# A gated graph network and an attention layer on one core: the weight setup in pieces among the first pair's work

## The chip, the cores and the metric

The kernel runs on one core of a Trainium2 chip. The metric is the time of one execution on the device in microseconds (us). Before the change it is 2468.5 us, the median of 3 runs (2468.18 to 2470.1). Five engines work beside each other, each in its own order: TensorE (PE) multiplies, VectorE (DVE) and ScalarE (ACT) work elementwise, GpSimd (POOL) does a few elementwise operations here, and SyncE (SP) issues DMAs. An engine waits at an instruction until what it needs from the others is there, and everything behind it on that engine waits too.

## The reference

There are 64 graphs of 256 nodes, with 256 features each. Layer 0 takes h = relu(layernorm(x)) and runs a gated recurrent cell three times; then x becomes x plus the last h:

```python
for i in range(3):
    m = h @ weight[i]                      # 256 x 256
    aggr = einsum('bst,bsd->btd', adj != 0, m)
    gi = aggr @ w_ih.T + b_ih ; gh = h @ w_hh.T + b_hh
    r = sigmoid(i_r + h_r) ; z = sigmoid(i_z + h_z)
    n = tanh(i_n + r * h_n)
    h = (1 - z) * n + z * h
```

Layer 1 is a graph attention with four heads on relu(layernorm(x)): a linear map W, b; logits from two attention vectors per head with a leaky relu; a mask where adj is not 1; a softmax over the row; a product with the mapped features; and a second residual.

## The kernel before

A pair is two graphs, 512 nodes; there are 32 pairs. Features lie on the 128 partitions in two halves, k or c = 0 and 1. For each of the three steps of layer 0 the kernel gathers h along the edges (`gather`, L444), and multiplies h with the hidden weights and the gathered sums s with one matrix that holds message weight and input weight together (`product`, L464, called as rA, rB, zA, zB, nhA, nhB, niA, niB). The matmuls run in a fast float format, fp32r, and to keep precision each operand is split in parts: for activations a leading part (`h_hi`, `s_hi`, on ACT), a rest (`h_lo` on POOL, `s_lo` on DVE) and a difference (`h_d`, `s_d`, on DVE); for weights the parts a, bS (the rest times 4096) and b-a. An A product takes the parts a and bS, a B product the part b-a. The gates then follow: `lift` copies the A product on ACT, `join` adds the B product on DVE, `squash` is the tanh; `addA`, `addB`, `new`, `diff` (POOL), `mixz` and `state` form the next h.

The order of the work is written out by hand. `PLAN` gives each operation of a pair a place, pairs follow each other at 74.0 (`PERIOD`), and all operations are emitted in the order of their places. There is no scheduler: on each engine the instructions stand in this order. Two or three pairs are under way at any time.

Ahead of all pairs stands the setup (L180 to L277). It loads the weights on ACT's DMA queue, transposes w_ih and w_hh on PE (L204, copies at L205), splits the hidden weights (`in_halves`, L183 to L193), then for each of the three steps transposes the message weights (L218), multiplies them with w_ih in plain fp32 (L224), copies the product to SBUF (L228) and splits it. At the end it makes the weights and biases of layer 1 (L259 to L275). The two tiles of layer 1's map are w_val and b_val. Setup's tiles lie in a pool of their own, which is closed at L277; the pools `sb` and `small`, with nearly all tiles of the pairs, are opened after that and take the same space. So the first pair's load of x (L311) waits for setup's last readers there. PSUM is one pool of 8 banks, taken in turn by all products and transposes, setup's too.

Of the kernel before, what the change touches and what calls it, by code (L numbers as in the profile page):

```python
# [17 lines left out]
P = 128  # L18
# [8 lines left out]
S = 4096.0  # L27
# [78 lines left out]


@with_exitstack
def gated_gnn_then_gat_kernel(
# [60 lines left out]

    setup_scope = ExitStack()
    setup = setup_scope.enter_context(tc.tile_pool(name="setup", bufs=1))

# [6 lines left out]
    w_msg = setup.tile([P, L, KD, D], F32, name="w_msg")  # L180
    nc.scalar.dma_start(w_msg, weight.rearrange("l (k q) e -> q l k e", q=P))

    def in_halves(full, name):  # L183

        a = const.tile([P, KD, G * P], F32R, name=f"a_{name}")
        b = setup.tile([P, KD, G * P], F32, tag="b", name=f"b_{name}", bufs=2)
        bs = const.tile([P, KD, G * P], F32R, name=f"bs_{name}")
        ba = const.tile([P, KD, G * P], F32R, name=f"ba_{name}")
        nc.scalar.mul(a, full, TRIM)
        nc.vector.tensor_sub(b, full, a)  # L190
        nc.scalar.mul(bs, b, S)
        nc.vector.scalar_tensor_tensor(ba, a, -1.0 / S, b, op0=ALU.mult, op1=ALU.add)
        return {"a": a, "bS": bs, "b-a": ba}  # L193

    wT, gates = {}, {}
    for name, src in (("ih", w_ih), ("hh", w_hh)):
        nat = setup.tile([P, G, D], F32, name=f"{name}_nat")
        nc.scalar.dma_start(nat, src.rearrange("(g q) d -> q g d", q=P))
        wT[name] = setup.tile([P, KD, G * P], F32, name=f"{name}_T")
        for k in range(KD):  # L200
            for g0 in range(0, G, 3):
                pt = bank(f"pw_{name}_{k}_{g0}")
                for g in range(3):
                    nc.tensor.transpose(pt[:, ts(g, P)], nat[:, g0 + g, ts(k, P)], ident)  # L204
                nc.vector.tensor_copy(wT[name][:, k, g0 * P : (g0 + 3) * P], pt[:, : 3 * P])  # L205

    for k in range(KD):
        nc.scalar.mul(wT["hh"][:, k, 2 * D :], wT["hh"][:, k, 2 * D :], 0.5)
    gates["h"] = in_halves(wT["hh"], "hh")


    for l in range(L):
        w_in = setup.tile([P, KD, G * P], F32, tag="w_in", name=f"w_in_{l}", bufs=2)
        msgT = setup.tile([P, KD, D], F32, tag="msgT", name=f"msgT_{l}", bufs=2)
        for e in range(KD):
            pt = bank(f"pmT_{l}_{e}")
            for d in range(KD):
                nc.tensor.transpose(pt[:, ts(d, P)], w_msg[:, l, d, ts(e, P)], ident)  # L218
            nc.scalar.copy(msgT[:, e, :], pt[:, :D])
        for d in range(KD):  # L220
            for g0 in range(0, G, 3):
                pt = bank(f"pwi_{l}_{d}_{g0}")
                for e in range(KD):
                    nc.tensor.matmul(  # L224
                        pt[:, : 3 * P], msgT[:, e, ts(d, P)], wT["ih"][:, e, g0 * P : (g0 + 3) * P],
                        start=(e == 0), stop=(e == KD - 1),
                    )
                nc.vector.tensor_copy(w_in[:, d, g0 * P : (g0 + 3) * P], pt[:, : 3 * P])  # L228
        gates[l] = in_halves(w_in, f"in{l}")

    bi = const.tile([P, G], F32, name="bi")
    bh = const.tile([P, G], F32, name="bh")
    nc.scalar.dma_start(bi, b_ih.rearrange("(g q) -> q g", q=P))
    nc.scalar.dma_start(bh, b_hh.rearrange("(g q) -> q g", q=P))
    nc.vector.tensor_scalar_mul(bh[:, 2 * KD :], bh[:, 2 * KD :], 0.5)

    brz = const.tile([P, 2 * KD], F32, name="brz")
    nc.vector.tensor_add(brz, bi[:, : 2 * KD], bh[:, : 2 * KD])
    nc.vector.tensor_scalar_mul(brz, brz, 0.5)

    w_nat = setup.tile([P, KD, D], F32, name="w_nat")
    nc.scalar.dma_start(w_nat, W.rearrange("(k q) d -> q k d", q=P))
    bcol = const.tile([P, KD], F32, name="bcol")
    nc.scalar.dma_start(bcol, b.rearrange("(k q) -> q k", q=P))

    a_exp = setup.tile([P, KD, 2 * H], F32, name="a_exp")
    nc.vector.memset(a_exp, 0.0)
    for h in range(H):
        k, q0 = divmod(h * C, P)
        for s in range(2):  # L250
            nc.scalar.dma_start(
                a_exp[q0 : q0 + C, k, s * H + h : s * H + h + 1],
                a[h : h + 1, s * C : (s + 1) * C].rearrange("o c -> c o"),
            )
    w_val = const.tile([P, KD, VW], F32, name="w_val")
    for k in range(KD):
        pt = bank(f"pwv_{k}")
        for g in range(KD):
            nc.tensor.transpose(pt[:, ts(g, P)], w_nat[:, g, ts(k, P)], ident)  # L259
        nc.vector.tensor_copy(w_val[:, k, :D], pt[:, :D])  # L260
        pa = bank(f"pwa_{k}")
        for g in range(KD):
            nc.tensor.matmul(
                pa[:, : 2 * H], w_nat[:, g, ts(k, P)], a_exp[:, g, :], start=(g == 0), stop=(g == KD - 1)
            )
        nc.vector.tensor_copy(w_val[:, k, D:], pa[:, : 2 * H])
    b_val = const.tile([P, VW], F32, name="b_val")
    nc.scalar.dma_start(b_val[:, :D], bass.AP(tensor=b.tensor, offset=b.offset, ap=[[0, P], [1, D]]))
    bmat = setup.tile([P, KD, P], F32, name="bmat")
    pb = bank("pb")  # L270
    for k in range(KD):
        nc.vector.tensor_copy(bmat[:, k, :], bcol[:, k : k + 1].to_broadcast([P, P]))
    for k in range(KD):
        nc.tensor.matmul(pb[:, : 2 * H], bmat[:, k, :], a_exp[:, k, :], start=(k == 0), stop=(k == KD - 1))
    nc.vector.tensor_copy(b_val[:, D:], pb[:, : 2 * H])  # L275

    setup_scope.close()  # L277
    sb = ctx.enter_context(tc.tile_pool(name="sb", bufs=2))
    small = ctx.enter_context(tc.tile_pool(name="small", bufs=3))
# [11 lines left out]
    class Pair:  # L291
# [26 lines left out]
        def reload(self):  # L318
            p = self.p
            self.x1 = sb.tile([P, R, D], F32, tag="x1", name=f"x1_{p}")  # L320
            nc.sync.dma_start(self.x1, x_rows[ts(p, T), :].rearrange("(r q) d -> q r d", q=P))
# [136 lines left out]
        def product(self, name, kind, sources, g):  # L458

            pt = bank(f"p{name}_{self.p}")  # L460
            pairs_ = (("a", "a"), ("bS", "b")) if kind == "A" else (("b-a", "d"),)
            parts = [(w[v], x, half, k) for w, x in sources for k in range(KD) for v, half in pairs_]
            for j, (w, x, half, k) in enumerate(parts):
                nc.tensor.matmul(  # L464
                    pt, w[:, k, ts(g, P)], self.halves[x, half, k], start=(j == 0), stop=(j == len(parts) - 1)
                )
            return pt
# [81 lines left out]
        def valadd(self, r):  # L549
            self.val = self.once("val", lambda: sb.tile([P, R, VW], F32, tag="val", name=f"val_{self.p}"))  # L550
            nc.vector.tensor_add(self.val[:, r, :], self.ps_["v", r][:, :VW], b_val)
# [7 lines left out]
        def srow(self):  # L559
            self.srow_ = tile_of("o", f"srow_{self.p}", bufs=1)  # L560
            nc.scalar.copy(self.srow_[:H, :], self.prow[:H, :])
# [5 lines left out]
        def rows(self, i):  # L567
            self.rows_[i] = sb.tile([P, H, N], F32, tag="rows", name=f"rows_{self.p}_{i}", bufs=1)
            src = self.line_[:, ts(i, N)]
            nc.sync.dma_start(self.rows_[i], bass.AP(tensor=src.tensor, offset=src.offset, ap=[[0, P], [T, H], [1, N]]))  # L570


        def slope(self, i, s):
            p, r = self.p, i * KN + s
            self.zz[r] = sb.tile([P, H, N], F32, tag="zz", name=f"zz_{p}_{r}")
# [39 lines left out]
        def prcopy(self, i, s, j):  # L615
            self.prT[i] = self.once(
                ("prT", i), lambda: sb.tile([P, KN, H, N], F32, tag="prT", name=f"prT_{self.p}_{i}", bufs=1)
# [17 lines left out]
        def ocopy(self, i):  # L635
            self.oT[i] = sb.tile([P, H // 2, N], F32, tag="oT", name=f"oT_{self.p}_{i}", bufs=1)
            nc.scalar.copy(flat(self.oT[i]), self.ps_["o"])
# [9 lines left out]
        def scale(self, i):  # L647
            self.o[i] = tile_of("o", f"o_{self.p}_{i}", bufs=1)
# [20 lines left out]
    todo = sorted(  # L669
        ((p * PERIOD + place, j, q, name, args) for p, q in enumerate(pairs) for j, (place, name, *args) in enumerate(PLAN)),  # L670
        key=lambda x: x[:2],
    )
    with tc.manual_schedule():
        for _, _, q, name, args in todo:
            if name[-1] in "AB" and name[:-1] in ("r", "z", "nh", "ni"):
                q.gate(name[:-1], name[-1], *args)
            else:
                getattr(q, name)(*args)
# [30 lines left out]
```

## Time and profile before

| | us |
|---|---|
| median of 3 runs | 2468.5 |
| the profiled execution, own time | 2469.03 |
| its span, first to last instruction | 2467.2 |
| PE busy | 2389.7 (97%) |
| DVE busy | 2111.5 (86%) |
| ACT busy | 1858.3 (75%) |
| POOL busy | 720.0 (29%) |

A page of the profile gives the busy time of each engine, the span in 40 slices with the clock that PE was granted, the DMA queues, the chain of work that ended last, and the costliest groups of instructions. A group's row names the line, the engine and the operation, what is written from what, the count, the busy time and the mean in ns, and the idle time ahead of it with what ended it. The chain of this kernel is PE for 94%, DVE for 3%, ACT for 2% and DMA for 1% of the span. The trace behind the page can be asked for a stretch of time: all instructions in order, who waited for whom, and busy times by stage.

### The profile page before, as it was taken

The numbers are of one execution on the slowest core, as the hardware profiler recorded it, in microseconds if no ns is written. First come the engines' busy times: TensorE is split into PE (matmuls) and PEld (weight loads), VectorE is DVE, ScalarE is ACT, GpSimd is POOL, SyncE is SP. The second block draws the span as 40 slices with busy tenths as digits, with TensorE's granted clock in tenths as the row PEclk, the third lists the DMA queues.
The fourth block names the chain that finished last, engine by engine and source line by source line (L and its number), as shares of the span: only waits on it lengthen the run. The fifth ranks groups of instructions, "written<-read, shape, count | busy, mean of one in ns | idle before, by whom it ended". The sixth has DMA issues, their size and how long they took to land.

```text
span 2467.2 us, 35760 instructions
## 1 busy us (share of the span) xinstructions
PE 2389.7 (97%) x12772; PEld 1933.8 (78%) x12772; DVE 2111.5 (86%) x3655; ACT 1858.3 (75%) x3985; POOL 720.0 (29%) x519
## 2 busy tenths in 40 slices
PE   5899999999999999999999999999999999999985
PEld 3678888888888888888888888888888888888863
DVE  5688988898988889988889898888998888989874
ACT  3458777778777778877777887777887777887765
POOL 0222323333332333232323233233333232323211
PEclk8999999999999999999999999999999999999997
DMA  2001111101111101111101111110111110111111
GB/s 79 26 1 48 50 50 52 33 29 49 51 48 52 52 26 36 48 48 52 52 26 35 48 52 48 52 44 23 47 48 48 52 52 27 35 48 48 35 35 35
DMA packets 107570, 105.98 MB, mean 43 GB/s; under 512 B 6272, under 2 KB 107264, under 8 KB 107392
## 3 DMA queue, kind: packets, MB, share of 16 engines
q1 hardware_dynamic: 102144, 100.94, 12.8%
q10 hardware_dynamic: 5248, 2.76, 0.4%
q8 instruction: 100, 1.64, 0.3%
q14 instruction: 78, 0.64, 0.1%
HBM read 86.65 MB, written 17.04 MB: 42 GB/s over the span
## 4 chain that ended last, share of the span: by engine, by line
PE 94%; DVE 3%; ACT 2%; DMA 1%; issue 0%; POOL 0%; ACTq 0%; POOLq 0%; DVEq 0%; SPq 0%
PE pzA L464 15%; PE prA L464 14%; PE pnhA L464 7%; PE pa L444 7%; PE pzB L464 7%; PE prB L464 7%; PE pniA L464 7%; PE po L630 5%; PE pv L545 4%; PE ppT L613 4%; PE pnhB L464 4%; PE pniB L464 3%; PE pn L389 3%; PE pt_b L366 1%; PE pt_a L366 1%; PE pob L643 1%
## 5 line engine op out<-in xcount | busy, mean ns | idle before, releaser
L422 POOL TENSOR_TENSOR hb<-h,ha 128x512 fp32r<-128x512 f32 x192 | 272.0, 1416 | 1116.1 <-ACT ha L418 724.2
L517 POOL TENSOR_TENSOR r<-h,h 128x512 f32<-128x512 f32 x192 | 285.7, 1494 | 235.4 <-ACT h L513 207.7
L598 ACT ACTIVATE zz<-zz,nmx 128x256 f32<-128x256 f32 x512 | 253.4, 499 | 15.6 <-DVE nmx L592 15.5
L577 ACT ACTIVATE zz<-rows,val 128x256 f32<-128x256 f32 x512 | 217.6, 500 | 9.0 <-DMA rows<-line 6.8
L486 DVE TENSOR_TENSOR z<-pzB,z 128x512 f32<-128x512 f32 x192 | 131.3, 684 | 95.9 <-PE pzB L464 50.6
L477 ACT ACTIVATE r<-prA 128x512 f32<-128x512 f32 x192 | 110.3, 593 | 115.7 <-PE prA L464 115.7
L444 PE MATMUL pa<-edge,nlo 128*128 128x256 f32 x768 | 193.1, 284 | 0.8 <-DVE nlo L410 0.4
L444 PE MATMUL pa<-edge,nhi 128*128 128x256 f32 x768 | 192.6, 283 | 0.2 <-ACT nhi L403 0.2
L494 ACT ACTIVATE z<-z,brz 128x512 f32<-128x512 f32 x192 | 137.6, 717 | 70.4 <-DVE z L486 70.4
L494 ACT ACTIVATE r<-r,brz 128x512 f32<-128x512 f32 x192 | 134.8, 719 | 71.5 <-DVE r L486 71.5
L656 POOL TENSOR_TENSOR o<-o,x 128x512 f32<-128x512 f32 x64 | 95.9, 1498 | 259.9 <-DVE shift_a L345 142.1
L464 PE MATMUL prA<-ha,a_hh 128*128 128x512 f32 x384 | 168.7, 439 | 0.0
L584 DVE SCALAR_TENSOR_TENSOR zz<-noedge,zz 128x1024 f32<-128x1024 int8 x128 | 156.0, 1219 | 12.0 <-ACT zz L577 11.9
L418 ACT ACTIVATE ha<-h 128x512 fp32r<-128x512 f32 x192 | 120.1, 626 | 58.1 <-DVE h L525 57.1
L498 DVE SCALAR_TENSOR_TENSOR r<-r,hs 128x512 f32<-128x512 f32 x192 | 127.1, 688 | 39.8 <-ACT r L494 39.7
L464 PE MATMUL pnhA<-ha,a_hh 128*128 128x512 f32 x384 | 155.9, 406 | 4.1 <-ACT ha L418 4.1
L464 PE MATMUL pniA<-sa,a_in 128*128 128x512 f32 x384 | 159.9, 416 | 0.0
L422 DVE TENSOR_TENSOR sb<-pa,sa 128x512 fp32r<-128x512 f32 x192 | 131.2, 683 | 32.9 <-ACT sa L418 32.9
L525 DVE SCALAR_TENSOR_TENSOR h<-r,h 128x512 f32<-128x512 f32 x192 | 157.6, 847 | 0.1
L464 PE MATMUL pzA<-ha,a_hh 128*128 128x512 f32 x384 | 157.4, 410 | 0.0
L513 ACT ACTIVATE h<-r,bi 128x512 f32<-128x512 f32 x192 | 135.2, 720 | 29.2 <-DVE r L508 25.3
L592 DVE TENSOR_REDUCE nmx<-zz 128x4 f32<-128x1024 f32 x128 | 154.5, 1207 | 1.2
(131 smaller groups left out, 7203.3 us busy)
## 6 DMA issues: line engine op xcount, KB each, us to landing
x<-in_x_dram SPq DMA_DIRECT2D x64, 512.0 KB, 5.4
rows<-line SPq DMA_DIRECT2D x64, 512.0 KB, 4.2
adj<-in_adj_dram SPq DMA_DIRECT2D x32, 512.0 KB, 5.0
out_dram<-o SPq DMA_DIRECT2D x64, 256.0 KB, 2.1
w_msg<-in_L_gnn_weight_dram ACTq DMA_DIRECT2D x1, 768.0 KB, 4.9
ih_nat<-in_L_gnn_w_ih_dram ACTq DMA_DIRECT2D x1, 768.0 KB, 6.7
hh_nat<-in_L_gnn_w_hh_dram ACTq DMA_DIRECT2D x1, 768.0 KB, 8.7
line<-srow SPq DMA_DIRECT2D x32, 8.0 KB
```

Source lines behind the costliest of these rows:

```text
L422: engine.tensor_sub(b, src, self.halves[x, "a", k])
L444: nc.tensor.matmul(pt[:, ts(i, N)], y[:, r, ts(e, P)], self.edge[:, r, :], start=(j == 0), stop=(j == len(parts) - 1),)
L464: nc.tensor.matmul(pt, w[:, k, ts(g, P)], self.halves[x, half, k], start=(j == 0), stop=(j == len(parts) - 1))
L486: nc.vector.tensor_add(v, self.ps_[kind, "B", c], v)
L494: nc.scalar.activation(v, v, AF.Tanh, bias=brz[:, g : g + 1], scale=0.5)
L513: nc.scalar.activation(n, self.g_["r", c], AF.Tanh, bias=bi[:, g : g + 1])
L517: nc.gpsimd.tensor_sub(self.g_["r", c], self.h_[l, c], self.h_[l + 1, c])
L525: nc.vector.scalar_tensor_tensor(n, self.g_["r", c], 0.5, n, op0=ALU.mult, op1=ALU.add)
L577: nc.scalar.activation(self.zz[r][:, h, :], self.rows_[i][:, h, :], AF.Prelu, bias=self.val[:, r, D + h : D + h + 1], alpha=ALPHA,)
L584: nc.vector.scalar_tensor_tensor(self.zz[r], self.noedge[:, r, :][:, None, :].to_broadcast([P, H, N]), MASKED, self.zz[r], op0=ALU.mult, o ...
L592: nc.vector.tensor_reduce(self.nmx[r], self.zz[r], AX.X, ALU.max, negate=True)
L598: nc.scalar.activation(self.zz[r][:, h, :], self.zz[r][:, h, :], AF.Exp, bias=self.nmx[r][:, h : h + 1], accum_out=self.den[r][:, h : h + 1],)
```

## The change

The setup becomes operations with places of their own in a second list, `START`, which is merged with the pairs' places. Its numbers are on the same scale: 0.0 is the first product of pair 0's first step, 47.84 that of its second, 97.96 that of its third.

- All setup loads move to SP's queue, behind pair 0's load of x and around its load of adj.
- Weights are handled in three pieces: the r and z columns of k = 0, those of k = 1, and the n columns of both. Each piece fills a PSUM bank and is split from there: `leading` on ACT, `rest`, `scaled` and `difference` on DVE. The copies of w_hh and of the products to SBUF, and `scaled` on ACT, are gone.
- The pieces of the hidden weights and of step 0 stand ahead of pair 0's first products. The message transposes and products of step 1 stand around its first `niA` and `niB`, those of step 2 between the second step's gathers and `nhA`; `layer1_weights`, whose instructions are those of L256 to L275 without the loads, stands between the second step's first rA and rB. `turned`, `hh`, `ih` and `ih_copy` transpose and copy as L200 to L205 did, in pieces.
- `sb` and `small` are opened ahead of setup's pool, so layer 0's tiles lie apart from it. A pool `late`, opened when setup's closes (place 70.0), holds tiles of layer 1 (x1, val, o, rows, zz, prT, oT).

```diff
+START = [
+    (-54.9, "load_ih"), (-54.8, "load_msg", 0), (-45.0, "load_hh"), (-44.9, "load_biases"),
+    (-44.8, "load_msg", 1), (-44.7, "load_msg", 2), (-44.6, "load_layer1"),
+    (-30.0, "ih", 0), (-29.9, "ih", 1), (-29.8, "ih", 2), (-29.7, "msg", 0), (-29.6, "hh", 2), (-29.5, "hh", 0),
+    (-29.4, "hh", 1), (-19.4, "ih_copy", 0), (-19.3, "ih_copy", 1), (-19.2, "ih_copy", 2), (-18.5, "msg_copy", 0),
+    (-16.0, "biases"),
+    (-17.9, "leading", "h", 2), (-17.8, "rest", "h", 2), (-17.7, "scaled", "h", 2), (-17.6, "difference", "h", 2),
+    (-16.4, "leading", "h", 0), (-16.3, "leading", "h", 1),
+    (-14.5, "rest", "h", 0), (-14.4, "rest", "h", 1), (-14.3, "scaled", "h", 0), (-14.2, "scaled", "h", 1),
+    (-14.1, "difference", "h", 0), (-14.0, "difference", "h", 1),
+    (-13.3, "product", 0, 0), (-13.2, "product", 0, 1), (-13.1, "product", 0, 2),
+    (-11.0, "leading", 0, 0), (-10.9, "leading", 0, 1), (-10.8, "leading", 0, 2),
+    (-10.7, "rest", 0, 0), (-10.6, "rest", 0, 1), (-10.5, "scaled", 0, 0), (-10.4, "scaled", 0, 1),
+    (-10.3, "difference", 0, 0), (-10.2, "difference", 0, 1),
+    (-2.0, "rest", 0, 2), (-1.9, "scaled", 0, 2), (-1.8, "difference", 0, 2),
+    (20.0, "msg", 1), (20.9, "msg_copy", 1), (24.0, "product", 1, 0), (24.1, "product", 1, 1), (24.2, "product", 1, 2),
+    (24.3, "msg", 2), (33.0, "leading", 1, 0), (33.1, "leading", 1, 1), (33.2, "leading", 1, 2), (33.3, "msg_copy", 2),
+    (38.0, "rest", 1, 0), (38.1, "rest", 1, 1), (38.2, "rest", 1, 2), (38.3, "scaled", 1, 0), (38.4, "scaled", 1, 1),
+    (38.5, "difference", 1, 0), (38.6, "difference", 1, 1), (38.7, "scaled", 1, 2), (38.8, "difference", 1, 2),
+    (41.0, "product", 2, 0), (41.1, "product", 2, 1), (41.2, "product", 2, 2),
+    (47.0, "leading", 2, 0), (47.1, "leading", 2, 1), (47.2, "leading", 2, 2),
+    (52.0, "rest", 2, 0), (52.1, "rest", 2, 1), (52.2, "rest", 2, 2), (52.3, "scaled", 2, 0), (52.4, "scaled", 2, 1),
+    (52.5, "difference", 2, 0), (52.6, "difference", 2, 1), (52.7, "scaled", 2, 2), (52.8, "difference", 2, 2),
+    (55.0, "layer1_weights"), (70.0, "close"),
+]
...
+    sb = ctx.enter_context(tc.tile_pool(name="sb", bufs=2))
+    small = ctx.enter_context(tc.tile_pool(name="small", bufs=3))
     setup_scope = ExitStack()
     setup = setup_scope.enter_context(tc.tile_pool(name="setup", bufs=1))
+    layer1 = {}
+
+    def late(*args, **kwargs):
+        return layer1["pool"].tile(*args, **kwargs)
...
-    w_msg = setup.tile([P, L, KD, D], F32, name="w_msg")
-    nc.scalar.dma_start(w_msg, weight.rearrange("l (k q) e -> q l k e", q=P))
...
+    NRZ = 2 * D
+    BLOCKS = ((0, slice(0, NRZ)), (1, slice(0, NRZ)), (None, slice(NRZ, G * P)))
+    class Weights:
+        def __init__(self, name, scale_n):
+            self.name, self.scale_n = name, scale_n
+            self.a, self.bs, self.ba = (
+                const.tile([P, KD, G * P], F32R, name=f"{x}_{name}") for x in ("a", "bS", "ba")
+            )
+            self.pt, self.b = {}, {}
+        def view(self, t, j):
+            k, cols = BLOCKS[j]
+            return t[:, :, cols] if k is None else t[:, k, cols]
+        def bank_view(self, t, j):
+            return t.rearrange("q (k n) -> q k n", k=KD) if BLOCKS[j][0] is None else t
+        def leading(self, j):
+            scale = self.scale_n if j == 2 else 1.0
+            nc.scalar.mul(self.view(self.a, j), self.bank_view(self.pt[j], j), scale * TRIM)
+        def rest(self, j):
+            scale = self.scale_n if j == 2 else 1.0
+            b = self.b[j] = setup.tile([P, NRZ], F32, tag="b", name=f"b_{self.name}_{j}", bufs=4)
+            nc.vector.scalar_tensor_tensor(
+                self.bank_view(b, j), self.bank_view(self.pt[j], j), scale, self.view(self.a, j),
+                op0=ALU.mult, op1=ALU.subtract,
+            )
+        def scaled(self, j):
+            nc.vector.tensor_scalar_mul(self.view(self.bs, j), self.bank_view(self.b[j], j), S)
+        def difference(self, j):
+            nc.vector.scalar_tensor_tensor(
+                self.view(self.ba, j), self.view(self.a, j), -1.0 / S, self.bank_view(self.b[j], j),
+                op0=ALU.mult, op1=ALU.add,
+            )
+    gates = {"h": Weights("hh", 0.5), **{l: Weights(f"in{l}", 1.0) for l in range(L)}}
...
+        def msg(self, l):
+            pt = self.pt["m"] = bank(f"pmT_{l}")
+            for e in range(KD):
+                for d in range(KD):
+                    nc.tensor.transpose(pt[:, e * D + d * P : e * D + (d + 1) * P], w_msg[l][:, d, ts(e, P)], ident)
...
+        def product(self, l, j):
+            k, cols = BLOCKS[j]
+            pt = gates[l].pt[j] = bank(f"pwi_{l}_{j}")
+            for n, d in enumerate(range(KD) if k is None else (k,)):
+                width = cols.stop - cols.start
                 for e in range(KD):
                     nc.tensor.matmul(
+                        pt[:, n * width : (n + 1) * width], self.msgT[l][:, e, ts(d, P)], ih_T[:, e, cols],
                         start=(e == 0), stop=(e == KD - 1),
                     )
...
+        def load_msg(self, l):
+            nc.sync.dma_start(w_msg[l], weight[l].rearrange("(k q) e -> q k e", q=P))
...
+        def layer1_weights(self):
...
+        def close(self):
+            setup_scope.close()
+            layer1["pool"] = ctx.enter_context(tc.tile_pool(name="late", bufs=2))
...
-            self.x1 = sb.tile([P, R, D], F32, tag="x1", name=f"x1_{p}")
+            self.x1 = late([P, R, D], F32, tag="x1", name=f"x1_{p}")
...
 
     pairs = [Pair(p) for p in range(NPAIR)]
-    todo = sorted(
-        ((p * PERIOD + place, j, q, name, args) for p, q in enumerate(pairs) for j, (place, name, *args) in enumerate(PLAN)),
-        key=lambda x: x[:2],
-    )
+    start = Setup()
+    todo = [(p * PERIOD + place, q, name, args) for p, q in enumerate(pairs) for place, name, *args in PLAN]
+    todo += [(place, start, name, args) for place, name, *args in START]
+    todo.sort(key=lambda x: x[0])
     with tc.manual_schedule():
...
```

## The prediction

> **What bounds the kernel now.** I read the page's slices first, for where TensorE (PE) is not full. The first line is PE's busy tenths, the second its granted clock; a slice is 61.7 us.
>
> ```profile
> PE   5899999999999999999999999999999999999985
> ...
> PEclk8999999999999999999999999999999999999997
> ```
>
> PE is short only in the first two slices and the last two. The stages say why: each row is a stretch in us, then busy time (instructions) of PE, weight loads, DVE, ACT and POOL, clock, DMA share, GB/s.
>
> ```profile
> 0.00:42.30 42.30, 25.36 (x100) 17.26 (x100) 25.08 (x39) 15.60 (x17) 0.74 (x7) 0.92 0.25 66
> 42.30:57.40 15.10, 4.92 (x25) 4.34 (x26) 5.42 (x15) 5.51 (x10) 2.60 (x2) 0.54 0.30 89
> 57.40:76.00 18.60, 17.33 (x74) 13.14 (x72) 10.39 (x15) 7.09 (x12) 1.27 (x1) 1.00 0.12 42
> 76.00:83.00 7.00, 0.22 (x2) 0.05 (x1) 5.36 (x8) 2.35 (x4) 2.48 (x2) 0.79 0.00 0
> 83.00:92.40 9.40, 8.14 (x36) 6.56 (x37) 6.97 (x18) 3.69 (x7) 3.76 (x3) 0.79 0.01 2
> 92.40:109.00 16.60, 16.60 (x85) 13.79 (x84) 11.02 (x18) 11.14 (x19) 2.81 (x3) 1.00 0.29 95
> 200.00:274.00 74.00, 74.00 (x402) 60.25 (x401) 65.77 (x116) 58.35 (x129) 23.32 (x17) 1.00 0.15 46
> ```
>
> From 200 us PE is busy 74.00 of 74.00; before 42.3 us there is setup alone, and the hole at 76 to 83 is the end of pair 0's first step. The timeline shows why pair 0 starts at 42.3:
>
> ```profile
> 40.42 1.76 DVE L192 SCALAR_TENSOR_TENSOR ba_in<-a_in,b_in 128x1536 fp32r<-128x1536 f32 x1
> 42.31 0.44 SPq L311 DMA_DIRECT2D x<-in_x_dram  x1
> ```
>
> The x tile lies in the setup pool's space, so its load waits for the last setup instruction. The chain of waits then runs through the load (42.31), four relus, the first gather, and into PE's gates at 62.17. A fixed mark for later: each pair issues one line DMA (SP's timeline).
>
> ```profile
> 260.82 0.27 SPq L565 DMA_DIRECT2D line<-srow  x1
> ...
> 334.09 0.27 SPq L565 DMA_DIRECT2D line<-srow  x1
> ...
> 407.23 0.27 SPq L565 DMA_DIRECT2D line<-srow  x1
> ```
>
> Pair 0's line stands at 187.62 and the thirtieth at 2308.56: (2308.56 - 187.62) / 29 = 73.14 us a pair, with the first interval already 73.20. The steady state begins at once. The order in which both kernels' instructions stand on each engine shows that from pair 0's second-step z products on, instructions and waits are the same, save one-time waits for setup loads that are long done. So whatever shift is reached there should arrive whole at the end.
>
> [...] after the hole at 76, gather matmuls start 0.21 us apart at 86.07 and 0.12 apart from 86.92. [...] sd (SBUF only) takes 1.65 us beside POOL's hb at 57.8 and 0.69 without; noedge averages 1675 ns in steady state and takes 0.69 alone. [...] here edge, 128x1024, takes 0.68 us, and a 128x512 tensor_tensor 0.68.
>
> **The change part by part.** Starts are spaced 0.60 us for a 512-wide DVE operation (two hs joins, 61.47 to 62.47 with their waits; pairs elsewhere take 1.28), 0.56 for ACT, 0.23 for a 512-column fp32r matmul.
>
> *Loads.* The setup loads go from ACT's to SP's queue in the order x, ih, first message matrix, adj, hh, then biases and the rest. The three 0.79 MB loads of before landed at 5.6, 7.9 and 10.5, so 0.79 MB costs 2.4 us and the first byte 2.5. That puts x at 4.8, ih at 7.2, the matrix at 8.0, adj at 9.7, hh at 12.1. SP has nothing else then; pair 1's x and adj come behind 20 setup loads (two bias loads of 2 us issue, eight of 0.6, the rest 0.5), at about 18, not needed until 60.
>
> *Start.* Statistics end at 7, but noedge stands ahead of the shift on DVE and waits for adj: shift at 10.6, three ih copies and edge to 13.0; relus and the message copy end on ACT at 13.2, the first hh piece's leading part at 13.8. Then DVE bounds. Until the last sd of the first step it has 6 rests, 6 differences and 6 pair operations (nlo apart) at 0.60 = 10.8, 6 scaled at 0.35 = 2.1, nlo 1.15, biases 0.25: 14.3, so 28.1; about 1 us of waits makes 29. ACT's nine copies and PE's products of 5.4 (as the 16 pwi rows at L224 take from 29.37, 5.43) fit beside. The first r product now starts at 29 against 62.0: **33 earlier**. This row has no twin before: scaled is at 0.35 by the edge row, at worst 0.60 (+1.5); two hb on POOL can stretch DVE by 1.3 each (+2.6); at best the waits vanish (-1).
>
> *First step, and its end.* Gates cost PE 14 in both. Four transposes (0.4) are added ahead of ni. The 7 us hole stays, because its chain (addA, addB, tanh, POOL diff, mixz, state) is unchanged; the three products of step 1 (5.4) and four transposes go into it for nothing. Without that cover they would cost 5.9. Naturals start at 51 against 82.96: **32 earlier**.
>
> *Second step.* ACT has three leading parts and a copy (2.2) behind ha and ahead of nhi: ACT is free at 82.96 before, so nhi comes 1 later relative to it: **31**. Products of step 2 (5.4) stand on PE between gather and nh. Before, PE waited there about 1.6 for ha and hb; the gather is now at full clock after products in the hole, and the wait is filled. nh at 61.7 against 88.4: **26.7**. On DVE stand, after nlo at 55.1: nine pieces of step 1 and one hd (5.3), sb, stats, hd, sd, rstd, noedge, sb (4.1), nine pieces of step 2 (4.65), sd (0.6), shift and four weight copies (0.95), two bmat copies (0.3): 71.0. Who waits: PE's b products for layer 1 need bmat, and prB, which stands behind them, needs that sd. PE finishes rA and layer 1's first products at 66.9 and waits until 71.0. prB at 71.0 against 94.31: **23.3**. The wait is 4.1[...]: minus 2, **21.3**. POOL's hb and pow (1.3 each) lie beside SBUF-only pieces: minus 1.3 to 2.6 in this stage or the first, I take 1.8: **19.5**. ACT's relus of pair 1 follow the same shift; before, shift came 1.4 ahead of prB, now 1.1, so nothing more is late behind it.
>
> *Removed or free.* fp32 hh and w_in copies go; layer 0's tiles stand apart from setup's, and the layer-1 tiles take setup's place after its last reader at 71; pair 0's second x load is not used until after its third step, some 35 us on.
>
> *Sum.* Profiled time 2469.03, span 2467.2, 1.83 around it. Span 2467.2 - 19.5 = 2447.7, profiled 2449.5. The median shown, 2468.5, is 0.5 below the profiled time: 2449.0.
>
> **The rivals.**
> 1. *DVE's pieces are dearer* (0.13). Twelve of the 18 scaled lie on binding stretches: 0.25 more each is 3.0. Four hb stretching by their full 1.28 rather than the 1.8 taken add 3.3, with hd and sd late behind them 1.5: gain 11.7, 2456.8. For it: the 1675 ns noedge. Against: alone these are 0.69 for twice the width.
> 2. *The pile is hidden* (0.11). If DVE's pieces start sooner, or step 2's do not hold bmat, prB starts right at 66.9, no half clock: 94.31 - 66.9 = 27.4, less 1.8 = 25.6: 2442.9. For it: DVE has 10.39 of 18.60 busy in the first step. Against: the pieces stand behind their products in the order.
> 3. *Nothing arrives* (0.03): x is still held, or the later pairs have their own bound: 2468.5. Against: no wait on x's load, PE full at 73.14 a pair.
> 4. *Slower* (0.03): all layer tiles move to other addresses, and DVE beside POOL there gets slower in every pair, through one engine that is 89% busy (65.77 of 74). Price 31 periods times d, less 19.5; zero at d = 0.63 us a pair, slower by 0.2% (4.9 us, about what a measurement tells from no change) from d = 0.79; at 1.0 it gives 2480. Against: no view shows a duration that depends on an address.
>
> **How the numbers follow.** The forecast has 0.70, for 2443 to 2457. It takes in +1.5 of scaled, -1 to +2.6 of POOL in the start, the half clock absent (-2) or longer (+1), and loads 2 us late. Rivals 1 and 2 lie on its two sides, and the range 2442 to 2459 holds most of both. Faster 0.70 + 0.13 + 0.11 = 0.94; same 0.03; slower 0.03.
>
> **What would show it.** First x load issued near 1 us; first r product near 29 (later if DVE is dearer); products of step 1 within the hole after the first ni; a PE wait of about 4 us between rA and rB of pair 0's second step, ended by DVE; pair 0's line DMA near 168; 73.14 us between lines after that. A line interval other than 73.1 to 73.2 would make the whole argument wrong; a line DMA near 176 or 162, the steps at DVE.

## The result

The changed kernel takes 2436.69 us, the median of 4 runs (2434.31 to 2437.97), beside 2468.69 (2468.18 to 2470.1, 4 runs) for the kernel before on the same chip: a ratio of 0.9868, 95% interval 0.9851 to 0.9885. That is 32.0 us less, where 19.5 were forecast; 2436.7 lies below the forecast range. The profiled execution has a span of 2432.5 us; it is the fastest of the four.

The page's slices after, PE's busy tenths and its granted clock (a slice is now 60.8 us): the second slice is full now, and the first has 7 where it had 5.

```profile
PE   7999999999999999999999999999999999999985
...
PEclk9999999999999999999999999999999999999997
```

The stages of the changed kernel, columns as in the prediction's table:

```profile
0.00:42.30 42.30, 31.77 (x144) 25.11 (x145) 26.36 (x54) 17.82 (x30) 5.71 (x10) 0.96 0.40 115
42.30:57.40 15.10, 12.35 (x48) 8.63 (x47) 11.82 (x20) 7.14 (x13) 5.07 (x4) 0.81 0.00 0
57.40:76.00 18.60, 17.24 (x81) 13.14 (x80) 16.30 (x38) 9.40 (x16) 2.33 (x2) 0.97 0.00 1
200.00:274.00 74.00, 73.94 (x408) 60.28 (x405) 66.12 (x115) 58.22 (x126) 23.93 (x17) 1.00 0.14 44
```

Up to 42.3 us, where before only setup ran, pair 0's first step is done. The last row looks much as before; in the same 74 us PE has 408 instructions where it had 402. A pair has 396 of them, so the shorter period found below makes some 2 of these 6; for the others the window falls elsewhere in a pair. SP's timeline shows both parts of the gain, first x's load, which no longer waits, and then the line DMAs of pairs 0, 1, 2 and 27:

```profile
0.74 0.44 SPq L417 DMA_DIRECT2D x<-in_x_dram  x1
...
164.26 0.34 SPq L671 DMA_DIRECT2D line<-srow  x1
...
237.21 0.27 SPq L671 DMA_DIRECT2D line<-srow  x1
...
309.95 0.27 SPq L671 DMA_DIRECT2D line<-srow  x1
...
2128.30 0.27 SPq L671 DMA_DIRECT2D line<-srow  x1
```

The same view of the kernel before has pair 27 here:

```profile
2162.14 0.27 SPq L565 DMA_DIRECT2D line<-srow  x1
```

Pair 0's line (line 0 from here on) stands at 164.26 instead of 187.62: 23.36 us. From pair 1 to pair 27 a pair took (2162.14 - 260.82) / 26 = 73.13 us before and takes (2128.30 - 237.21) / 26 = 72.73 now. In those 26 periods 10.2 us are gained, in the first interval 0.25, and behind pair 27's line the remaining 0.9; all together the spans' difference of 34.7. So there are two gains: the start, which was forecast, and a faster pace of every pair, which was not.

Where the pace comes from is read by groups. In a period the 216 gate matmuls (L464, now L570) take 52.20 us from start to start before and 51.76 after; `pa` takes 0.04 more, and every other kind of matmul the same within 0.005. Some 195 of the 216 have no wait behind them and save 3.2 ns each (the table of eight kernels below), which is 0.6 us; the others, with a wait or a change of shape behind them, give some 0.2 back. Instructions and waits are in the same order in both kernels there. One group of each shows it (minimum, median and maximum ns), first before, then after:

```profile
L464 PE MATMUL pnhA<-hb,bs_hh x312: 392/396/397, 300.0 to 2199.7; 128*128 128x512 f32 x156
```

```profile
L570 PE MATMUL pnhA<-hb,bS_hh x316: 387/389/398, 299.8 to 2192.7; 128*128 128x512 f32 x158
```

What differs is where tiles lie in SBUF. The small bias tiles, w_val and b_val are now allocated ahead of the gates' weights, so the weights start at byte 20352 of each partition instead of 17056. Layer 0's tiles of the pairs stay where they were (adj at 94080 in both); a few tiles of layer 1 move by 768 bytes.

### The profile page after: what moved, and what is told of

Read it like the earlier page. It is cut to its first block, busy times and chain, and to the rows that moved or that the text cites. A ratio compares the mean times of both kernels' runs of the same rounds, so it can differ in the third digit from the quotient of the medians.

```text
span 2432.5 us, 35764 instructions
## 1 busy us (share of the span) xinstructions
PE 2373.7 (98%) x12772; PEld 1934.1 (80%) x12772; DVE 2106.6 (87%) x3666; ACT 1851.0 (76%) x3984; POOL 723.4 (30%) x519
## 4 chain that ended last, share of the span: by engine, by line
PE 84%; DVE 12%; ACT 2%; DMA 1%; issue 0%; POOL 0%; SPq 0%; POOLq 0%; DVEq 0%; ACTq 0%
PE prA L570 14%; PE pzA L570 12%; PE prB L570 7%; PE pa L550 6%; PE pnhA L570 6%; PE pzB L570 5%; PE pniA L570 5%; PE po L736 5%; PE pv L651 5%; PE ppT L719 4%; PE pn L495 4%; PE pnhB L570 4%; DVE zz L690 3%; PE pniB L570 2%; DVE nmx L698 2%; DVE r L608 2%
## 5 line engine op out<-in xcount | busy, mean ns | idle before, releaser
L570 PE MATMUL prA<-ha,a_hh 128*128 128x512 f32 x384 | 167.7, 437 | 0.0
L570 PE MATMUL pnhA<-ha,a_hh 128*128 128x512 f32 x384 | 154.7, 403 | 4.3 <-ACT ha L524 4.3
L570 PE MATMUL pniA<-sa,a_in 128*128 128x512 f32 x384 | 158.6, 413 | 0.0
L570 PE MATMUL pzA<-ha,a_hh 128*128 128x512 f32 x384 | 156.8, 408 | 0.0
```

The lines of the kernel that those rows point to most:

```text
L570: nc.tensor.matmul(pt, w[:, k, ts(g, P)], self.halves[x, half, k], start=(j == 0), stop=(j == len(parts) - 1))
```

## The experiments on the pace

**Does the weights' place do it, and by which rule?** The first theory was that the weights' start must be a multiple of 64 bytes. Four kernels moved only tiles. In the first, one bias tile goes ahead of the weights of the kernel before (17088, a multiple of 64):

```diff
+    bi = const.tile([P, G], F32, name="bi")     # ahead of the weights
...
-    bi = const.tile([P, G], F32, name="bi")     # was behind them
```

> The kernel before with one tile (bi, 32 bytes a partition with padding) allocated ahead of the gates' weights, so that the nine hidden and input weight tiles and the others start at a multiple of 64 bytes instead of 32 above one; every other tile keeps its address, the order of instructions is that of before. Theory A (the weights' place decides the pace of the gates' matmuls): 72.73 us between line DMAs, gates' matmuls 227 to 231 ns apart, pair 0's line near 186.9, time near 2456.5. Rival B (the pace comes from the order of setup, the queues or layer 1's new places): 73.14 us between lines, time 2468.7.

It took 73.16 us a pair and 2471.2 us, ratio 1.0007 (1.0 to 1.0013). That theory fell. In the second, the changed kernel's brz goes behind its weights (20320):

```diff
-    brz = const.tile([P, 2 * KD], F32, name="brz")
     gates = {"h": Weights("hh", 0.5), ...}
+    brz = const.tile([P, 2 * KD], F32, name="brz")
```

> The changed kernel with brz allocated behind the weights, so that the weights start 32 above a multiple of 64, as before the change; every other tile and all instructions as in the changed kernel. Theory A: 73.14 us between lines, pair 0's line near 165.0, time near 2449, which is the forecast. Rival B: 72.73 between lines, time 2436.7.

It took 73.07 us a pair and 2447.87 us, ratio 0.9916 (0.9899 to 0.9932): 32 bytes take the pace away and leave the start. In the third, 32 bytes of padding behind the constants move all the pairs' tiles of the kernel before up, its weights staying at 17056; in the fourth, bi, bh and brz go ahead of its weights (17152):

```diff
+    pad = const.tile([P, 8], F32, name="pad")   # third: behind the weights
+    nc.vector.memset(pad, 0.0)
```

> The kernel before with 32 bytes of padding at the end of the constants: the weights stay at 32 above a multiple of 64, and all tiles of the pairs move there too. Theory A with the weights' own place: 73.14 us between lines. Rival A2, the place of weights relative to the moving operand: 72.73. Rival A3, any operand off a multiple of 64 costs: above 73.4.

> The kernel before with bi, bh and brz allocated ahead of the weights: they start at a multiple of 128 bytes rather than of 64 alone. Theory A with 64 as the grain: 72.73 us between lines, as with the multiple of 64. If 128 is the grain: this one at 72.73 and the multiple of 64 at 73.14, or this one faster still.

The third took 72.72 a pair with weights that were not moved at all, 2454.77 us in one run; the fourth 73.00, and 2465.64 in one run. So neither place alone counts. What the fast kernels have in common is the distance from weights to pair tiles: a multiple of 256 bytes. Two further kernels test that. In the fifth, a 32-byte tile of the kernel before goes behind the weights, which then start at 17024; the pair tiles stay. In the sixth, all four bias tiles of the changed kernel go behind its weights (20224), which makes the distance 128:

```diff
-    mhalf = const.tile([P, R], F32, name="mhalf")      # fifth: moved behind the weights
-    nc.gpsimd.memset(mhalf, -0.5)
```

> The kernel before with one small tile (mhalf, 32 B a partition) allocated behind the gates' weights instead of ahead: the weights start at 17024 instead of 17056, all tiles of the pairs stay. The distance from the weights to the pairs' tiles becomes a multiple of 256 B, as in the changed kernel and in the version whose pair tiles lie 32 B higher. Theory distance (the pace of a pair is set by that distance modulo 256 B): 72.7 us between lines, mean start-to-start of the gates' matmuls near 229.8 ns, line of pair 0 unmoved at 185 to 188, time 2455 to 2457. Rival place (what counts is where the pairs' own tiles lie, which the version with tiles 32 B higher moved): 73.1 us between lines and 2468 to 2470.

> The changed kernel with the four bias tiles (bi, bh, bcol, brz, 128 B) allocated behind the gates' weights: the weights start at 20224 instead of 20352, all pair tiles stay; the distance modulo 256 B becomes 128. w_val and b_val move down by 96 B. Theory distance: as for the kernel before at 128 (73.00 us), 72.95 to 73.1 between lines, time 2443 to 2447. Rival (only distances that are odd multiples of 32 B are slow): 72.73 and 2436 to 2438.

SP's timeline of the fifth, pairs 0, 1 and 27:

```profile
186.95 0.34 SPq L565 DMA_DIRECT2D line<-srow  x1
259.95 0.27 SPq L565 DMA_DIRECT2D line<-srow  x1
...
2151.54 0.27 SPq L565 DMA_DIRECT2D line<-srow  x1
```

Its start is that of the kernel before; then a pair takes (2151.54 - 259.95) / 26 = 72.75. It ran in 2458.39 us, ratio 0.9955 (0.9941 to 0.997). The sixth took 73.00 a pair and 2444.09 us in one run. All eight kernels together, by weights' start less pair tiles' start, modulo 256 bytes:

| kernel | distance | us a pair | mean of gate matmuls, start to start, ns |
|---|---|---|---|
| changed kernel | 0 | 72.73 | 229.8 |
| before, pair tiles 32 higher | 0 | 72.72 | 229.8 |
| before, weights 32 lower | 0 | 72.75 | 229.9 |
| before | 32 | 73.13 | 233.0 |
| before, weights at 17088 | 64 | 73.16 | 233.3 |
| before, weights at 17152 | 128 | 73.00 | 232.4 |
| changed, weights at 20224 | 128 | 73.00 | 232.4 |
| changed, weights at 20320 | 224 | 73.07 | 232.8 |

(The mean leaves out matmuls that are 245 ns or more ahead of the next, which wait or change shape.) The two gains multiply: 0.9955 for the distance alone and 0.9916 for the change without it give 0.9871, against 0.9868 for the whole.

**Who gets in whose way?** A kernel of its own computes nothing of the reference: 120 matmuls for each of 13 distances, all run twice, beside elementwise work on SBUF tiles that PE never reads.

```diff
+for beside in (False, True):
+    for dw, dm in ((0, 0), (8, 0), (16, 0), (24, 0), (32, 0), (40, 0), (48, 0), (56, 0), (64, 0), (0, 8), (8, 8), (0, 32), (32, 32)):
+        for b in range(15):
+            ...                                # beside: 3 on DVE, 3 on ACT, every other time 1 on POOL
+            for j in range(8):
+                w, m = ((w0, m0), (w1, m1))[j % 2]
+                o = dw + 128 * (j // 2)
+                nc.tensor.matmul(pt, w[:, o : o + 128], m[:, dm : dm + 512], start=(j == 0), stop=(j == 7))
```

> Not the reference's computation: fp32r matmuls of 128x128 weights with 512 columns, 120 for each of 13 distances between moving tile and weights (0, -32, -64, -96, -128, -160, -192, -224, -256, 32, 0 with both 32 higher, 128, 0 with both 128 higher), first with PE alone, then with plain elementwise work of 512 columns running on DVE, ACT and POOL, on tiles that PE never reads. Theory one (the conflict is between TensorE's own reads, of the next weights and of the moving tile): the spacing of matmuls depends on the distance already with PE alone, lowest at 0, -256 and where both moved, 1 to 2% higher elsewhere. Theory two (other engines' accesses are needed for it): PE alone shows one spacing for all, and the second part differs by distance. Theory three (the distance alone is not what counts): no part differs by distance.

Nothing ties the other engines to PE, so they ran ahead at once: the first pass was the one beside them, and the end of the second had PE alone. The stages show it. The first two rows are weights 256 bytes up and moving tile 32 up, beside DVE and ACT; the last three are the same two and "both 32 up", with PE alone:

```profile
242.70:269.80 27.10, 27.10 (x120) 22.17 (x119) 25.84 (x38) 25.80 (x42) 0.00 (x0) 1.00 0.00 1
269.90:297.80 27.90, 27.90 (x123) 22.64 (x122) 26.57 (x40) 26.56 (x43) 0.00 (x0) 1.00 0.00 1
...
603.00:630.20 27.20, 27.20 (x120) 22.26 (x119) 0.00 (x0) 0.00 (x0) 0.00 (x0) 1.00 0.00 1
630.20:658.20 28.00, 28.00 (x123) 22.74 (x122) 0.00 (x0) 0.00 (x0) 0.00 (x0) 1.00 0.00 1
658.20:685.40 27.20, 27.20 (x120) 22.25 (x120) 0.00 (x0) 0.00 (x0) 0.00 (x0) 1.00 0.00 1
```

From start to start a matmul took, in both passes alike (the first distance in the first pass, 227.1, apart):

| weights less moving tile, bytes | ns |
|---|---|
| 0, 256, 0 with both 32 up, 0 with both 128 up | 226.7 |
| 192 | 228.9 |
| 128 | 232.4 |
| 32, 64, 160, 224, -32, -128 | 233.3 |
| 96 | 234.3 |

That is what the first theory of the three expected: the distance acts with no other engine at work (226.7 against 233.3), and as a distance, since at 0 moving both tiles changes nothing (226.7). Modulo 256 is not the whole of it: 128 and -128 differ by 0.9. The kernels' own means at 32, 64 and 128 (233.0, 233.3, 232.4) are these values within 0.3 ns. At 0 the kernels have 229.8, not 226.7: their gates take only half of what the alignment gives here. What holds the other 3 ns was not tried; in the kernels other engines also read PSUM, and here none does. That TensorE's own reads of weights and moving tile conflict, as the theory has it, was not shown; the runs show the dependence of the spacing on the distance alone.

## The experiments on the start

**What was moving the products worth?** First everything of steps 1 and 2, and layer 1's weights, ahead of pair 0's first products; then the same with layer 1's weights left in their place:

```diff
-    (24.0, "product", 1, 0), ... (41.0, "product", 2, 0), ... (55.0, "layer1_weights"),
+    (-12.8, "product", 1, 0), ... (-9.1, "product", 2, 0), ... (-1.3, "difference", 2, 2),
+    (-1.2, "layer1_weights"),                  # first kernel; second: (55.0, "layer1_weights")
```

> The changed kernel with products and pieces of steps 1 and 2 and layer 1's weights ahead of pair 0's first products, so that only the early x load, the pieces and the tiles apart are left of the change. Theory (DVE bounds the start: 18 more pieces of 0.35 to 0.60 us, and the four copies): first r product 9 to 11 later than 28.33, at 37.5 to 39.5; the hole after the first n product stays empty; no product between gather and nh, no layer 1 product between rA and rB, so most comes back: second step's first B product at 71.5 to 73 against 70.17, time 2438 to 2440. Rival (moving the products behind the first slot saves their PE and DVE time for good): second step's first B product near 80, time 2446 to 2448. In both the pace of 72.73 a pair stays.

> The changed kernel with products and pieces of steps 1 and 2 ahead of pair 0's first products, and layer 1's weights left at 55.0. Theory (both engines' work ahead of the first slot delays it, and only what no longer stands in the second step comes back): first B product of r near 46 to 48 against 30.17, since the second sd stands behind step 2's pieces; the second step's first B product near 80 to 82 against 70.17, for the product between gather and nh (6.3) and the wait on bmat (1.4) are gone; line of pair 0 at 173 to 176, time 2446 to 2449. Rival (DVE's pile in the second step was the bound, and taking it away returns nearly all): second step's first B product at 71 to 74, time 2438 to 2440. The pace of 72.73 a pair stays in both.

The first took 2449.76 us, ratio 0.9919 (0.9905 to 0.9934), its pace 72.74 a pair, line 0 at 177.80; first B product of r at 55.07, the second step's at 85.04. Neither number of the theory held, and its rival's 2446 to 2448 were just passed. PE's waits from 20 to 85 us say why: layer 1's weights stand on PE ahead of the gates, and their bmat (the bias copied across, which layer 1's bias product `pb` reads) stands on DVE behind all the pieces.

```profile
PE pn L495 <- DVE h L631: 6.8, 1, 6.8
PE pb L378 <- DVE bmat L376: 5.8, 1, 5.8
PE pwa L369 <- DVE b_in L253: 2.4, 1, 2.4
```

The first line is the hole, empty again. Without that misplacement the second kernel took 2445.69 us, ratio 0.9899 (0.9882 to 0.9915), line 0 at 173.32; first B product of r at 46.61, the second step's at 80.33, both as its theory said. PE's wait here is for `sb`; it stands on DVE behind step 2's pieces, and those behind a gather that stood on PE behind all products (DVE's timeline):

```profile
36.24 0.69 DVE L528 TENSOR_TENSOR sb<-pa,sa 128x512 fp32r<-128x512 f32 x1 [5.04 <-ACT sa L524]
...
45.54 0.68 DVE L528 TENSOR_TENSOR sb<-pa,sa 128x512 fp32r<-128x512 f32 x1
```

So moving the products of steps 1 and 2 is worth 2445.69 - 2436.69 = 9.0 us of the start (9.06 by line 0; 7.7 by the two ratios, each against its own runs of the kernel before); the first B product of r goes back by 16.4, and only 6.3 of it return up to that of the second step, for want of what no longer stands there. The rest of the start's gain is what is left of the change in that kernel: early loads, tiles apart, pieces. It is some 12 us by the medians (32.0 less 11.4 of the pace and 9.0) and 187.62 - 173.32 = 14.3 by line 0; the three were not taken apart.

**Can layer 1's weights go into the hole too?**

```diff
-    (55.0, "layer1_weights"), (70.0, "close"),
+    (24.4, "layer1_weights"), (70.0, "close"),
```

> The changed kernel with layer 1's weights made at place 24.4, in the hole after the first n product, instead of 55.0 between the second step's rA and rB. Theory (PE's 3.14 us between the end of rA at 67.03 and the B product at 70.17 are layer 1's products, 1.3, and a wait on DVE's bmat, 1.4): DVE has four copies and two bmat less ahead of sd, so the B product starts 1.3 to 2.0 sooner behind rA, and the time falls to 2434.5 to 2435.5. Rival (layer 1's copies on DVE stand ahead of the first step's state chain in the hole and hold it up): the naturals of the second step start 1 to 1.5 later than 49.4, and the time stays at 2436 to 2438.

It is slower than the changed kernel: 2441.39 us, ratio 0.9887 (0.9871 to 0.9904), line 0 at 169.77 (5.5 later). The rival's mechanism is right, and it costs 7.3 us where 1 to 1.5 were expected. On DVE the copies of w_val stand ahead of addB (L614), the head of the chain that the hole waits for, and they wait for PE to finish the products of step 1:

```profile
41.54 0.69 DVE L608 SCALAR_TENSOR_TENSOR r<-pniA,r 128x512 f32<-128x512 f32 x1
47.80 0.42 DVE L366 COPY w_val<-pwv 128x256 f32<-128x256 f32 x1 [5.58 <-PE pwv L365]
...
50.26 1.28 DVE L614 TENSOR_TENSOR r<-pniB,r 128x512 f32<-128x512 f32 x2
```

addB starts at 50.26 instead of 42.98, and the naturals at 56.67 instead of 49.40: all 7.3 us. The products of step 1 are free in this hole because nothing of theirs stands on DVE there.

**Is the wait on bmat only a place in a queue?** Its two copies go ahead of step 2's pieces:

```diff
-    (55.0, "layer1_weights"), (70.0, "close"),
+    (51.9, "bias_copies"), (55.0, "layer1_weights"), (70.0, "close"),
```

> The changed kernel with the two bmat copies (0.36 us on DVE) placed at 51.9, ahead of the rests of step 2, instead of behind the four w_val copies at 68.55 to 69.36. Theory (PE's 1.36 us before layer 1's bias product is a wait on the order of DVE's queue alone): that wait goes, the second step's first B product starts 1.2 to 1.5 sooner behind the end of rA, now with sd (done at 68.5) just in time; time 2435 to 2435.5. Rival (DVE is full there, so the copies ahead make sd late by as much): the wait moves from bmat to sd, and the time stays within 0.5 of 2436.7.

The wait on bmat is gone and stands in the next place, at the B product, 2.02 us long. What ends it is DVE's first copy of w_val, which stands behind the last sd: the B product is given the PSUM bank that this copy reads.

```profile
PE prB L573 <- DVE w_val L371: 2.0, 1, 2.0
```

```profile
68.51 0.69 DVE L535 SCALAR_TENSOR_TENSOR sd<-sb,sa 128x512 fp32r<-128x512 f32 x1
...
69.18 0.42 DVE L371 COPY w_val<-pwv 128x256 f32<-128x256 f32 x1
```

sd ends at 69.20, the copy at 69.60, and the B product starts at 69.66 against 70.17. So the wait has moved along DVE's queue, as the rival said, if one place further than sd. Yet the kernel took 2433.2 us (2432.41 to 2434.67, 4 runs), ratio 0.9849 (0.9834 to 0.9863), 3.5 below the changed kernel's median; the two intervals overlap, and the two did not run side by side. In the profiles its line 0 is 1.7 earlier. At 90 us it is still 1.0 later (pair 1's first B product of r at 90.50 against 89.49); the 2.7 are gained from there to 100, at the naturals (`pn`, transposes of h) of the third step, which the edit does not touch. First the changed kernel, then this one:

```profile
90.00:108.00 18.00, 15.05 (x66) 12.34 (x65) 10.07 (x15) 7.27 (x12) 2.56 (x2) 0.81 0.00 0
```

```profile
90.00:108.00 18.00, 15.05 (x78) 12.43 (x78) 12.25 (x18) 7.79 (x13) 2.75 (x3) 1.00 0.00 0
```

After a 3.0 us wait for h (2.9 here) PE was granted 0.81 of its clock in one execution and all of it in the other. The edit is not needed for that: the second and the sixth kernel above have the changed kernel's order, a wait of 2.8 us at this place, and in their profiles a clock of 1.00 from 86 to 108 us. Nor is it an accident of one profile alone: the clock averaged over an execution is 0.990 or 0.991 in all four of this kernel's and 0.988 or 0.989 in all four of the changed kernel's. Whether the edit makes the full clock likelier stays open. It is the fastest kernel measured, by a margin that is not settled.

## Why the prediction was wrong

The working of the start held in the main; the step from there to the end did not.

- *x waits for setup's space*: right. Its load was issued at 0.74 (forecast near 1).
- *First r product at 29*: 28.33. POOL's second hb beside DVE took 2.66 us (the first 1.27) and held PE 2.2, so POOL's stretch, which the sum placed here or in the second step, was already in this number. That pow would hold DVE as hb does was the author's estimate and was not shown: in the kernel before, noedge took 0.69 at 48.54, with pow beside it from 48.78 on.
- *The hole takes step 1's products for nothing*: right; they lie at 42.43 to 47.6, and PE then waits 1.2 for h. Naturals at 49.40, forecast 51.
- *The gather is at full clock after products in the hole*: wrong. PE's waits and timeline of the changed kernel, first the waits from 20 to 85 us:

```profile
PE pnhA L570 <- POOL hb L528: 2.2, 1, 2.2
PE pa L550 <- ACT nhi L509: 1.4, 1, 1.4
PE pb L378 <- DVE bmat L376: 1.4, 1, 1.4
PE pn L495 <- DVE h L631: 1.2, 1, 1.2
```

```profile
54.06 0.41 PE L550 MATMUL pa<-edge,nlo 128*128 128x256 f32 x1
54.27 0.41 PE L550 MATMUL pa<-edge,nhi 128*128 128x256 f32 x1
...
55.98 6.62 PE L311 MATMUL pwi<-ih_T,msgT 128*128 128x512 f32 x16
62.26 0.58 PE L570 MATMUL pnhA<-ha,a_hh 128*128 128x512 f32 x1
...
69.73 0.58 PE L378 MATMUL pb<-a_exp,bmat 128*128 128x8 f32 x4 [1.36 <-DVE bmat L376]
70.17 0.71 PE L570 MATMUL prB<-hd,ba_hh 128*128 128x512 f32 x2
```

  Gathers start 0.21 us apart, at a granted clock of 0.50 (53.50 to 55.98), and 16 products take 6.28 at 0.79, where 16 took 5.16 in the hole at 1.00. Between the products of the hole and the gather there are only transposes and two waits of 1.2 and 1.4; with which of these the lower clock came, the trace does not tell.
- *A wait of 4.1 ahead of the B product, and half clock after it*: the wait was 1.36, and PE was granted 1.00 of its clock from 70.17 to 84. The 2 taken off for half clock was the author's estimate: the kernel before had a clock of 0.51 from 82.9 to 87.0, behind a wait of 6.8, and no trace shows that a wait of 4.1 brings it. The bmat copies end at 69.7, 1.3 earlier than worked out, and PE, slowed as above, came 1.5 later. The B product itself starts at 70.17 (forecast 71.0): 24.1 earlier than before. A lower clock did cost 1.2, in another place: from the naturals of the third step behind their wait to the next n product, pair 1's, PE takes 13.7 us, before 12.5. That stretch of the kernel before had a clock of 0.91, against 0.81 above:

```profile
114.00:132.00 18.00, 15.22 (x72) 12.49 (x71) 10.62 (x16) 7.17 (x12) 2.56 (x2) 0.91 0.00 0
```

  With 0.4 more by line 0 the start gains 24.1 - 1.2 + 0.4 = 23.3 in the profiled execution, not 19.5: 0.8 from the B product, 0.8 from the clock, 0.4 behind it, and the 1.8 taken off for POOL, which the 24.1 already contain. Single executions differ, though: in the profiles of the second and the sixth kernel, with the same order, line 0 stands at 161.49 and 165.14. By the medians, 32.0 less some 11.4 of the pace leaves 20.6, and the changed kernel with its pace taken away gave a ratio of 0.9916, or 20.7 us (22.1 by the two medians; some 1.8 of it pace, at 73.07 a pair against 73.13). So by the medians the start was forecast to about 1 us, and with either figure, 20.6 or 23.3, it alone would have left the time within the range.
- *"Whatever shift is reached there should arrive whole at the end"*: this step failed. It took the pace of 73.14 us for a property of the order of instructions, which stayed the same. The pace fell by 0.40 us in each of some 29 periods, because the change allocates small tiles ahead of the weights.
- *Rival 4, "no view shows a duration that depends on an address"*: true of one kernel's views, and no argument. One kernel has one address for each tile, so its profile cannot show such a dependence. The rival named the moved tiles and got the sign and the engine wrong: it is PE, and it got faster. The forecast's own mark, a line interval other than 73.1 to 73.2, came true at 72.73.
- Rivals 1 and 3 did not occur: DVE's pieces cost what was taken for them (scaled 0.43 and 0.33), and the start arrived. Rival 2 came true by half: PE did wait for bmat, but 1.36 us and not 4.1, and the clock behind it was 1.00.

## What to carry to other kernels

Before a change that adds, drops or reorders allocations is costed, compare the addresses of weights and moving tiles modulo 256 bytes in both kernels, if their matmuls are like these: one 32-byte tile moved here gave 72.75 us a pair instead of 73.13, a ratio of 0.9955 in time. A mark that counts periods, such as one DMA per pair, parts a gain at the start from a gain in the pace at a glance, and the two then want separate causes. When work is put into an idle stretch of one engine, look at its helpers on the engine that the stretch is waiting for: 1.3 us of layer 1's products on PE, with copies on DVE, made the hole 7.3 us longer.

## What was not expected of the hardware

In the kernel of matmuls alone, fp32r matmuls of 512 columns with new weights for each started 226.7 ns apart where weights and moving tile lay a multiple of 256 bytes apart, and 228.9 to 234.3 ns apart at the other distances tried, with PE alone as with DVE and ACT busy. The spacing was not symmetric: 228.9 at 192 bytes, 233.3 at 64. The `pv` of the two kernels compared, plain fp32 with 264 columns, took 222 ns from start to start at distances of 64, 96 and 128 alike; a distance of 0, where a gain would show, was not tried. And a wait for h of 2.8 to 3.0 us, at the same place, was followed by half clock in the changed kernel's profile (0.50 from 93.6 to 98, 0.81 over 18 us) and by full clock in those of three near relatives (1.00 over those 18 us with the early bias copies, 1.00 from 86 to 108 in the second and the sixth kernel).
